# A four-layer graph network: the last LSTMs of two groups of nodes computed together by seven products

## The chip, the cores and the metric

The kernel runs on one core of one Trainium2 chip. The metric is device microseconds from the start to the end of one execution, as the median of several runs.

## The reference

The input x has the shape (128, 64, 256): 128 graphs of 64 nodes with 256 features. All graphs share one adjacency matrix of 64 x 64. Four layers follow each other, each of the form layernorm(x + layer(x)). Layer 0 is a chain of three graph convolutions, layer 1 a convolution in the basis of eigenvectors, layer 3 attention along the edges. Layer 2 holds what is changed:

```python
h = relu(einsum('ts,bsh->bth', adj, x @ Wg0 + bg0))
h = relu(einsum('ts,bsh->bth', adj, h @ Wg1 + bg1))
for p in range(1, 5):
    nw = 64 // p
    wins = h[:, :nw * p, :].reshape(B * nw, p, 256)
    last = lstm_last(Wih[p - 1], Whh[p - 1], bih[p - 1], bhh[p - 1], wins)   # p steps, gates i, f, g, o
    h = h.at[:, arange(nw) * p + (p - 1), :].set(last.reshape(B, nw, 256))
```

So four LSTMs run one after the other on the nodes of a graph. The one with number p takes windows of p neighbouring nodes, runs p steps along each window, and writes its last hidden state over the window's last node. The next one reads what the one before has written. A step multiplies the input, and from the second step on the hidden state too, with a matrix of 256 x 1024, which gives four gates of 256. All of it is done in float32.

## The kernel before

The 8192 rows are cut into 16 groups of 512 rows (8 graphs of 64 nodes). Layer 0 and the eigenvectors come first, for all groups. After them the first stage's memory is given back, the LSTMs' weights are loaded, and layers 1 to 3 run.

For layers 1 to 3, `unit(groups)` writes down the operations of one or two groups: `layer1`, then `to_lstm` with the two convolutions, the four LSTMs, `from_lstm`, and `layer3`. A planner (`Plan.run`) holds up to four units at a time (`UNITS = 4`) and puts their operations into the order of each engine: among the operations that could start earliest by its own table of durations, it takes the one that is due first. The order is fixed when the program is built, and each engine then follows its own list. Work tiles come from pools of fixed size: `WIDE = 7` tiles of 1024 columns (tag `w`), `NARROW = 3` of 512, `GATES = 6` of 1024 for the gates, `CELLS = 3` and `OUTS = 4` of 512 columns for cell state and hidden state (`c`, `hs`), and 8 banks of PSUM. An operation that needs a tile waits in the plan until one is free. When no unit is left to start and `LASTS` groups or fewer are open, TensorE takes the group with the most operations left first.

The units are pairs of groups up to group 12, and then the last four groups one by one (`SINGLE = 4`). The profile counts groups from 1 here: groups 13 to 16 are single units.

In `to_lstm` each group gets its hidden state `hT`, a `w` tile with two halves of 128 features (index k) by 64 nodes by 8 graphs. There are two ways to run an LSTM step.

- `lstm(hT, p, first, nw)` runs one group alone. For each gate and each half of 128 outputs, TensorE sums two products of 128 x 128 by n columns for the input and two for the hidden state in one bank; ScalarE takes the gate's tanh straight from the bank. n is 8 windows' columns: 168 for the third LSTM (21 windows), 128 for the fourth (16 windows).
- `fast(p, n, x, ...)` takes the columns in two halves (index w) and uses seven products in place of eight for each gate, in Winograd's form of Strassen's scheme on 2 x 2 blocks: output halves by feature halves by column halves. VectorE first makes four differences of the inputs (`T1` to `T4`), and the same of the hidden states. The products go to three banks; ScalarE copies three partial sums out of a bank, VectorE adds three more, and then the tanh follow. The weights' sums (`S1` to `S4`) are made once, by `add_weights`.

The first and the second LSTM (`singles`, `pairs`) use `fast` with two halves of one group. The third runs by `lstm(hT, 3, 0, 21)` for each group, the fourth by `four(hTs)` for a pair, which calls `fast` with the two groups as the column halves, and by `lstm(hTs[0], 4, 0, 16)` for a single unit. For the groups in `ENDING`, the last two, `from_lstm` and `layer3` use transposes on TensorE; for the others the data are turned by way of DRAM (`across`).

Of the kernel before, what the change touches and what calls it, by code (L numbers as in the profile page):

```python
# [11 lines left out]
F32 = mybir.dt.float32  # L12
# [740 lines left out]
P = 128  # L753
D = 256
EPS = 1e-5
UNITS = 4
ENDING = (14, 15)
WIDE = 7
NARROW = 3
GATES = 6  # L760
ATT = 2
CELLS = 3
OUTS = 4
LASTS = 3
PERIOD = 17.0
SINGLE = 4
FARS = 8
# [60 lines left out]
def kernel(  # L828
# [346 lines left out]
    for i in range(4):  # L1175
        wih.append(load(wb, f"wih{i}", c_ih[i], "(k p) f -> p k f", [P, 2, 1024], p=P))
        whh.append(load(wb, f"whh{i}", c_hh[i], "(k p) f -> p k f", [P, 2, 1024], p=P) if i else None)
# [31 lines left out]
    def quarters(w):  # L1209
        w = w.rearrange("p k (q h m) -> p k q h m", q=4, h=2)  # L1210
        return [w[:, k, :, h] for h in range(2) for k in range(2)]

    ways = {}
    SPARE21 = {(1, 0), (2, 0), (2, 1)}

    def add_weights(p, ready):
        ways[p] = []
        names = "igo" if p == 1 else "ifgo"
        for k, w in enumerate((wih[p - 1], whh[p - 1])):
            if w is None:  # L1220
                continue
            spare21 = (p, k) in SPARE21
            s = wb.tile([P, 4 - spare21, len(names), P], F32, name=f"sums{p}{k}")
            s, w = plan.tile("sums", [P, 4 - spare21, len(names), P], s), plan.tile("sums", [P, 2, 1024], w)
            whole = quarters(w)
            for at, to in ((slice(0, 1), slice(0, 1)), (slice(2, 4), slice(1, 3))) if p == 1 else ((slice(0, 4),) * 2,):
                a11, a12, a21, a22 = (x[:, at] for x in whole)
                S1, S2, S4, S3 = [s[:, j, to] for j in range(4 - spare21)] + [a21] * spare21
                V.tensor_add(S1, a21, a22, ready=ready)
                V.tensor_sub(S2, S1, a11, ready=ready)  # L1230
                V.tensor_sub(S4, a12, S2, ready=ready)
                V.tensor_sub(S3, a11, a21, ready=ready)
            raw = [{q: x[:, "ifgo".index(q)] for q in names} for x in whole]
            sums = [{q: s[:, j, i] for i, q in enumerate(names)} for j in range(4 - spare21)] + [raw[2]] * spare21
            ways[p].append([raw[0], raw[1], raw[3], sums[0], sums[1], sums[3], sums[2]])

# [14 lines left out]
    def work():  # L1251
        return plan.tile("w", [P, 1024])
# [4 lines left out]
    def ps4(shape=(P, 512)):  # L1257
        return plan.tile("ps", shape)
# [61 lines left out]
    def to_lstm(xs, there):  # L1320
# [19 lines left out]
        pairs(hT)  # L1340
        lstm(hT, 3, 0, 21)
        return hT
# [139 lines left out]

    def lstm(hT, p, first, nw):

        n = 8 * nw
        wi, wh, bias = wih[p - 1], whh[p - 1], cbi[:, p - 1, :]
        hs = None
        for t in range(p):  # L1490
            rows = slice(first + t, first + t + (nw - 1) * p + 1, p)
            xt = [hT[:, k, rows, :] for k in range(2)]
            last = t == p - 1
            names = "figo" if t else "igo"
            gate = []
            for h in range(2):
                G = plan.tile("gates", [P, 1024])[:, :len(names) * n].rearrange("p (q n) -> p q n", n=n)
                gate.append({q: G[:, i] for i, q in enumerate(names)})
            if not t:
                c = plan.tile("c", [P, 512])[:, :2 * n].rearrange("p (h n) -> p h n", h=2)  # L1500
            new = None if last else plan.tile("hs", [P, 512])[:, :2 * n].rearrange("p (h n) -> p h n", h=2)
            for h in range(2):
                for q in names:
                    j = 2 * "ifgo".index(q) + h
                    m = slice(j * P, (j + 1) * P)
                    pp = ps4()[:, :n]
                    ins = [(wi[:, k, m], xt[k]) for k in range(2)]
                    outs = [(wh[:, k, m], hs[:, k, :]) for k in range(2)] if t else []
                    if t and h == 0 and q in names[:2]:

                        run(pp, ins, last=False)
                        run(pp, outs, first=False)
                    else:
                        run(pp, ins + outs)
                    S.activation(gate[h][q], pp, AF.Tanh, bias=bias[:, j:j + 1], scale=0.5 if q == "g" else 0.25)
                    if q == "g":
                        to = gate[h]["g"] if t else c[:, h, :]
                        if t:
                            V.scalar_tensor_tensor(c[:, h, :], gate[h]["f"], 1.0, c[:, h, :], op0=ALU.add,
                                                   op1=ALU.mult)  # L1520
                        V.scalar_tensor_tensor(to, gate[h]["i"], 1.0, gate[h]["g"], op0=ALU.add,
                                               op1=ALU.mult)
                        if t:
                            V.scalar_tensor_tensor(c[:, h, :], c[:, h, :], 0.5, to, op0=ALU.mult, op1=ALU.add)
                        S.activation(gate[h]["i"], c[:, h, :], AF.Tanh, scale=0.5)
                    if q == "o" and not last:
                        V.scalar_tensor_tensor(new[:, h, :], gate[h]["o"], 1.0, gate[h]["i"], op0=ALU.add,
                                               op1=ALU.mult)
            if p == 4 and t == 2:
                plan.late = plan.ops[-1]  # L1530
            if last:

                for h in range(2):
                    V.scalar_tensor_tensor(hT[:, h, slice(first + p - 1, first + nw * p, p), :],
                                           gate[h]["o"].rearrange("p (w b) -> p w b", b=8), 1.0,
                                           gate[h]["i"].rearrange("p (w b) -> p w b", b=8), op0=ALU.add,
                                           op1=ALU.mult)
            hs = new

    def fast(p, n, x, hs=None, c=None, new=None, write=None):  # L1540
# [20 lines left out]
        ins = [x] if first else [x, [[parts(hs[:, k, w]) for w in range(2)] for k in range(2)]]  # L1561
        T = work()[:, :4 * n * len(ins)].rearrange("p (s i n) -> p s i n", s=len(ins), i=4)
        T1, T2, T3, T4 = ([parts(T[:, s, i]) for s in range(len(ins))] for i in range(4))
        for s, b in enumerate(ins):
# [58 lines left out]

    def state(tag):
        return plan.tile(tag, [P, 512]).rearrange("p (h w n) -> p h w n", h=2, w=2)

    def turn_out(dst, o, t):
        V.scalar_tensor_tensor(dst, o.rearrange("p (r b) -> p r b", b=8), 1.0, t.rearrange("p (r b) -> p r b", b=8),
                               op0=ALU.add, op1=ALU.mult)

# [16 lines left out]

    def four(hTs):

        def write(h, o, t):  # L1650
            for w in range(2):
                turn_out(hTs[w][:, h, 3:64:4, :], o[:, w], t[:, w])

        c, hs = state("c"), None
        for t in range(4):
            x = [[hTs[w][:, k, t:t + 61:4, :] for w in range(2)] for k in range(2)]
            new = state("hs") if t < 3 else None
            fast(4, 128, x, hs, c, new, write)
            if t == 2:
                plan.late = plan.ops[-1]  # L1660
            hs = new

    def unit(groups):

        if groups[0] == 0:
            add_weights(1, 10.0)
            add_weights(2, 30.0)
            add_weights(4, 60.0)
        there, hTs = [], []
# [15 lines left out]
        plan.group = groups[0] + 1  # L1685
        if len(groups) == 2:
            four(hTs)
        else:
            lstm(hTs[0], 4, 0, 16)
        late = plan.late  # L1690
# [10 lines left out]

    spare[0] = lambda: tl(few, [P, D], "spare")

    def left_over():
# [54 lines left out]
```

## Time and profile before

| | us |
|---|---|
| median of 3 runs | 2362.1 |
| lowest and highest run | 2360.63, 2365.0 |
| the profiled execution | 2365.63 |
| its span, first to last instruction | 2363.8 |
| TensorE (PE) busy | 2313.2 |
| VectorE (DVE) busy | 1630.6 |
| ScalarE (ACT) busy | 1137.4 |
| mean granted TensorE clock | 0.992 |

In the profile PE is TensorE's matrix product and PEld its weight load. A float32 product of the program shows as two records on PE. Nearly all operations are recorded by helpers, so that most lines read L162 (the planner's `emit`) or L963 (layer 0); groups are told apart by tiles and shapes. "x1408" is the number of records, and the two numbers after a bar are busy microseconds and the mean nanoseconds of one. In the chain and in the timeline the first number of a line is the start in microseconds, the second the duration.

### The profile page before, as it was taken

What the parts mean: (1) busy time and instruction counts of PE and PEld (TensorE: products, weight loads), DVE (VectorE), ACT (ScalarE), POOL (GpSimd) and SP (SyncE); (2) the same over time, 40 slices, a digit from 0 to 9 for tenths busy, and PEclk for the clock granted to TensorE, in tenths of its full rate; (3) what the DMA queues carried; (4) which work ended last, traced back from release to release, by engine and by line L of the source; (5) the groups of instructions that cost most, each with busy time, mean ns of one, the idle gap of its engine ahead of it and who ended that gap; (6) DMA issues with size and microseconds to landing.
All of it is one profiled execution on the core that took longest, in us unless ns stands there. A gap on an engine that the chain in (4) does not pass through costs nothing.

```text
span 2363.8 us, 50357 instructions
## 1 busy us (share of the span) xinstructions
PE 2313.2 (98%) x19872; PEld 2035.5 (86%) x19872; DVE 1630.6 (69%) x5562; ACT 1137.4 (48%) x2838; POOL 142.8 (6%) x315
## 2 busy tenths in 40 slices
PE   8999999999999999999999999999999999999996
PEld 6877888887787778999899899899999998998995
DVE  6888887778898557558567666756755858567535
ACT  2333343333333346555546545545556455545544
POOL 0000000000000010001000100100000101011002
PEclk9999999999999999999999999999999999999998
DMA  7000000000000040002111211220210312222001
GB/s 236 10 1 10 19 10 10 10 10 10 11 10 10 1 161 13 16 11 72 54 42 55 81 51 39 80 65 32 81 43 32 120 48 66 66 92 84 19 1 48
DMA packets 79837, 108.08 MB, mean 46 GB/s; under 512 B 23280, under 2 KB 63984, under 8 KB 79600
## 3 DMA queue, kind: packets, MB, share of 16 engines
q1 hardware_dynamic: 79248, 104.58, 13.3%
q8 instruction: 156, 2.56, 0.4%
q14 instruction: 81, 0.66, 0.1%
q10 hardware_dynamic: 352, 0.28, 0.0%
HBM read 57.90 MB, written 45.09 MB: 44 GB/s over the span
## 4 chain that ended last, share of the span: by engine, by line
PE 92%; DVE 5%; ACT 1%; issue 1%; POOL 0%; DMA 0%; SPq 0%; ACTq 0%; POOLq 0%; DVEq 0%
PE ps L162 60%; PE ps L963 30%; PE ps L1006 2%; DVE D L52 1%; DVE X L162 1%; PE pc L312 1%; DVE w L162 1%; DVE tw L52 0%; DVE st L162 0%; POOL rs L162 0%; DVE gates L162 0%; ACT gates L162 0%; DVE ss L52 0%; DVE v L162 0%; DMA XA<-in_x_dram 0%
## 5 line engine op out<-in xcount | busy, mean ns | idle before, releaser
L162 PE MATMUL ps<-w,wih 128*128 128x128 f32 (+2 forms) x3708 | 649.7, 299 | 3.2 <-DVE gates L162 1.7
L162 PEld LDWEIGHTS ps<-w,wih 128*128 128x128 f32 x3708 | 550.6, 191 | 33.0 <-issue 13.6
L162 ACT ACTIVATE gates<-ps,cbi 128x168 f32<-128x168 f32 (+2 forms) x722 | 261.5, 388 | 207.7 <-PE ps L162 204.1
L162 PE MATMUL ps<-w,sums 128*128 128x128 f32 (+1 forms) x2368 | 353.8, 289 | 3.0 <-ACT gates L162 2.0
L162 PE MATMUL ps<-hs,whh 128*128 128x128 f32 (+1 forms) x1952 | 343.2, 291 | 1.4 <-DVE hs L162 1.4
L162 PEld LDWEIGHTS ps<-w,sums 128*128 128x128 f32 x2368 | 307.6, 192 | 16.6 <-issue 4.3
L162 PEld LDWEIGHTS ps<-hs,whh 128*128 128x128 f32 x1952 | 288.3, 191 | 3.2 <-DVE hs L162 1.8
L162 ACT ACTIVATE gates<-gates,cbi 128x256 f32<-128x256 f32 (+2 forms) x500 | 214.3, 477 | 129.1 <-DVE gates L162 129.0
L162 DVE TENSOR_TENSOR gates<-gates,ps 128x512 f32<-128x512 f32 (+2 forms) x264 | 157.5, 601 | 164.1 <-PE ps L162 157.1
L963 PE MATMUL ps<-aw,h 128*128 128x256 f32 x1024 | 228.2, 380 | 0.0
L963 PEld LDWEIGHTS ps<-aw,h 128*128 128x128 f32 x1024 | 192.6, 190 | 25.9 <-issue 0.4
L162 ACT COPY gates<-ps 128x512 f32<-128x512 f32 (+2 forms) x264 | 136.8, 520 | 160.6 <-PE ps L162 158.8
L972 ACT ACTIVATE h<-h 128x512 f32<-128x512 f32 x128 | 80.6, 630 | 184.4 <-DVE h L52 184.2
L162 DVE SCALAR_TENSOR_TENSOR gates<-gates 128x256 f32<-128x256 f32 (+3 forms) x188 | 78.4, 418 | 69.9 <-ACT gates L162 69.6
L963 PE MATMUL ps<-aw,m 128*128 128x512 f32 x256 | 120.5, 612 | 0.9 <-ACT m L1010 0.9
L963 PE MATMUL ps<-m,aw 128*128 128x256 f32 x512 | 119.7, 387 | 1.0 <-ACT LV L385 0.6
L963 PE MATMUL ps<-ss,tw 128*128 128x256 f32 x512 | 117.8, 379 | 0.1
L963 PE MATMUL ps<-ss,aw 128*128 128x256 f32 x512 | 116.7, 379 | 0.0
L963 PEld LDWEIGHTS ps<-m,aw 128*128 128x128 f32 x512 | 98.1, 194 | 17.3 <-issue 3.0
L162 DVE SCALAR_TENSOR_TENSOR c<-gates,c 128x256 f32<-128x256 f32 (+2 forms) x156 | 56.6, 363 | 76.8 <-ACT gates L162 76.4
L963 PEld LDWEIGHTS ps<-ss,aw 128*128 128x128 f32 x512 | 96.8, 190 | 13.0
L162 POOL TENSOR_SCALAR rs<-mv 128x2 f32<-128x2 f32 x96 | 23.7, 256 | 1390.8 <-DVE mv L162 1372.1
(326 smaller groups left out, 3559.2 us busy)
## 6 DMA issues: line engine op xcount, KB each, us to landing
far<-w SPq DMA_DIRECT2D x42, 512.0 KB, 2.7
w<-far SPq DMA_DIRECT2D x168, 128.0 KB, 3.0
X<-rest SPq DMA_DIRECT2D x24, 512.0 KB, 3.3
out_dram<-X SPq DMA_DIRECT2D x64, 128.0 KB, 1.8
rest<-XA SPq DMA_DIRECT2D x12, 512.0 KB, 2.6
rest<-X SPq DMA_DIRECT2D x12, 512.0 KB, 2.8
XA<-in_x_dram SPq DMA_DIRECT2D x22, 256.0 KB, 6.0
wih<-in_c_ih_dram SPq DMA_DIRECT2D x4, 1024.0 KB, 7.7
```

The costliest lines, as they stand in the source:

```text
L52: return getattr(self.engine, name)(out, *args, **kw)
L162: getattr(e, name)(*[real(x) for x in args], **{k: real(v) for k, v in kw.items()})
L312: PE.matmul(out, lhsT, rhs, start=True, stop=True)
L963: PE.matmul(out, lhsT, rhs, start=start, stop=stop)
L972: S.activation(dst, src, AF.Relu)
L1006: PE.matmul(p[h][m, k, t, :], src[hs, t, f], sqT2[hs, hs], start=True, stop=True)
```

## The change

All 16 groups now form pairs. The third LSTM leaves `to_lstm` and, like the fourth, is run for a pair by `long(hTs, p)`, which calls `fast` with the two groups as the two column halves (n = 168 or 128). `lstm` and `four` are gone. A later step of the third LSTM needs eight differences of 168 columns, more than one `w` tile holds, so `fast` takes two tiles there; with four gates of 168 columns it makes two passes of two gates each. There are nine `w` tiles in place of seven; cell and hidden state tiles are 672 columns wide and there are two of each. `LASTS` is 2 in place of 3. `add_weights` makes sums for all four LSTMs, always three new ones, the fourth in the place of one of the weights' quarters. The unused quarter of the first LSTM's input weights is no longer loaded, which makes two transfers of one. The output that nobody reads of layer 0's normalization (`spare`) goes into the tile of the fourth LSTM's sums.

```diff
-WIDE = 7
+WIDE = 9
-CELLS = 3
-OUTS = 4
-LASTS = 3
+CELLS = 2
+OUTS = 2
+LASTS = 2
-SINGLE = 4
...
+            wih.append(wb.tile([P, 2, 768], F32, name="wih0"))
+            for to, at, n in ((0, 0, 256), (256, 512, 512)):
+                nc.sync.dma_start(wih[0][:, :, to:to + n],
+                                  c_ih[0].rearrange("(k p) f -> p k f", p=P)[:, :, at:at + n])
...
+            s = wb.tile([P, 3, nq, P], F32, name=f"sums{p}{k}")
+            if p == 4:
+                spare[0] = lambda s=s: s[:, 0, 0:2, :].rearrange("p q n -> p (q n)")
...
+            V.tensor_add(S1, a21, a22, ready=ready)
+            V.tensor_sub(S2, S1, a11, ready=ready)
+            V.tensor_sub(S4, a12, S2, ready=ready)
+            V.tensor_sub(a21, a11, a21, ready=ready)
...
         singles(hT)
         pairs(hT)
-        lstm(hT, 3, 0, 21)
         return hT
...
-    def lstm(hT, p, first, nw):
...
-        T = work()[:, :4 * n * len(ins)].rearrange("p (s i n) -> p s i n", s=len(ins), i=4)
-        T1, T2, T3, T4 = ([parts(T[:, s, i]) for s in range(len(ins))] for i in range(4))
+        if 4 * n * len(ins) <= 1024:
+            T = work()[:, :4 * n * len(ins)].rearrange("p (s i n) -> p s i n", s=len(ins), i=4)
+            T = [T[:, s] for s in range(len(ins))]
+        else:
+            T = [work()[:, :4 * n].rearrange("p (i n) -> p i n", i=4) for _ in ins]
+        T1, T2, T3, T4 = ([parts(v[:, i]) for v in T] for i in range(4))
...
-    def state(tag):
-        return plan.tile(tag, [P, 512]).rearrange("p (h w n) -> p h w n", h=2, w=2)
+    def state(tag, n=128):
+        return plan.tile(tag, [P, 672])[:, :4 * n].rearrange("p (h w n) -> p h w n", h=2, w=2)
...
-    def four(hTs):
+    def long(hTs, p):
+
+        nw = 64 // p
+
+        def seen(h, w, t):
+            return hTs[w][:, h, t:t + (nw - 1) * p + 1:p, :]
 
         def write(h, o, t):
             for w in range(2):
-                turn_out(hTs[w][:, h, 3:64:4, :], o[:, w], t[:, w])
-
-        c, hs = state("c"), None
-        for t in range(4):
-            x = [[hTs[w][:, k, t:t + 61:4, :] for w in range(2)] for k in range(2)]
-            new = state("hs") if t < 3 else None
-            fast(4, 128, x, hs, c, new, write)
-            if t == 2:
+                turn_out(seen(h, w, p - 1), o[:, w], t[:, w])
+
+        c, hs = state("c", 8 * nw), None
+        for t in range(p):
+            x = [[seen(k, w, t) for w in range(2)] for k in range(2)]
+            new = state("hs", 8 * nw) if t < p - 1 else None
+            fast(p, 8 * nw, x, hs, c, new, write)
+            if p == 4 and t == 2:
                 plan.late = plan.ops[-1]
             hs = new
...
             add_weights(2, 30.0)
+            add_weights(3, 45.0)
             add_weights(4, 60.0)
...
-        if len(groups) == 2:
-            four(hTs)
-        else:
-            lstm(hTs[0], 4, 0, 16)
+        for p in (3, 4):
+            long(hTs, p)
...
-        units = [(g, g + 1) for g in range(0, NT // 4 - SINGLE, 2)] + [(g,) for g in range(NT // 4 - SINGLE, NT // 4)]
+        units = [(g, g + 1) for g in range(0, NT // 4, 2)]
```

More of the change, by code (lines that the diff above doesn't have):

```diff
@@ L1175 @@
     for i in range(4):
-        wih.append(load(wb, f"wih{i}", c_ih[i], "(k p) f -> p k f", [P, 2, 1024], p=P))
+        if i:
+            wih.append(load(wb, f"wih{i}", c_ih[i], "(k p) f -> p k f", [P, 2, 1024], p=P))
+        else:
[3 more added lines that the diff above has]
+                                  c_ih[0].rearrange("(k p) f -> p k f", p=P)[:, :, at:at + n])
         whh.append(load(wb, f"whh{i}", c_hh[i], "(k p) f -> p k f", [P, 2, 1024], p=P) if i else None)
@@ L1209, in quarters @@
     def quarters(w):
-        w = w.rearrange("p k (q h m) -> p k q h m", q=4, h=2)
+        w = w.rearrange("p k (q h m) -> p k q h m", h=2, m=P)
         return [w[:, k, :, h] for h in range(2) for k in range(2)]
     ways = {}
-    SPARE21 = {(1, 0), (2, 0), (2, 1)}
     def add_weights(p, ready):
@@ L1221, in add_weights @@
                 continue
[L1222 to L1235, printed above, removed]
+            nq = len(names)
+            s = wb.tile([P, 3, nq, P], F32, name=f"sums{p}{k}")
+            if p == 4:
+                spare[0] = lambda s=s: s[:, 0, 0:2, :].rearrange("p q n -> p (q n)")
+            s, w = plan.tile("sums", [P, 3, nq, P], s), plan.tile("sums", [P, 2, nq * 2 * P], w)
+            a11, a12, a21, a22 = whole = quarters(w)
+            S1, S2, S4 = (s[:, j] for j in range(3))
+            V.tensor_add(S1, a21, a22, ready=ready)
+            V.tensor_sub(S2, S1, a11, ready=ready)
+            V.tensor_sub(S4, a12, S2, ready=ready)
+            V.tensor_sub(a21, a11, a21, ready=ready)
+            raw = [{q: x[:, i] for i, q in enumerate(names)} for x in whole]
+            sums = [{q: s[:, j, i] for i, q in enumerate(names)} for j in range(3)]
+            ways[p].append([raw[0], raw[1], raw[3], *sums[:2], raw[2], sums[2]])
     def products(calls, also=(), **kw):
@@ L1481, in layer3 @@
                 Q.dma_start(out_t[:, at + j, :], x2[:, j, :])
-    def lstm(hT, p, first, nw):
[L1487 to L1512, printed above, removed]
-                    else:
[L1514 to L1538, printed above, removed]
@@ L1561, in fast @@
         ins = [x] if first else [x, [[parts(hs[:, k, w]) for w in range(2)] for k in range(2)]]
-        T = work()[:, :4 * n * len(ins)].rearrange("p (s i n) -> p s i n", s=len(ins), i=4)
-        T1, T2, T3, T4 = ([parts(T[:, s, i]) for s in range(len(ins))] for i in range(4))
+        if 4 * n * len(ins) <= 1024:
+            T = work()[:, :4 * n * len(ins)].rearrange("p (s i n) -> p s i n", s=len(ins), i=4)
+            T = [T[:, s] for s in range(len(ins))]
+        else:
+            T = [work()[:, :4 * n].rearrange("p (i n) -> p i n", i=4) for _ in ins]
+        T1, T2, T3, T4 = ([parts(v[:, i]) for v in T] for i in range(4))
         for s, b in enumerate(ins):
@@ L1622, in fast @@
                             write(h, g, gate[h]["i"])
-    def state(tag):
-        return plan.tile(tag, [P, 512]).rearrange("p (h w n) -> p h w n", h=2, w=2)
+    def state(tag, n=128):
+        return plan.tile(tag, [P, 672])[:, :4 * n].rearrange("p (h w n) -> p h w n", h=2, w=2)
     def turn_out(dst, o, t):
-        V.scalar_tensor_tensor(dst, o.rearrange("p (r b) -> p r b", b=8), 1.0, t.rearrange("p (r b) -> p r b", b=8),
-                               op0=ALU.add, op1=ALU.mult)
+        o, t = (v.rearrange("p (r b) -> p r b", b=8) for v in (o, t))
+        V.scalar_tensor_tensor(dst, o, 1.0, t, op0=ALU.add, op1=ALU.mult)
     def singles(hT):
@@ L1685, in unit @@
         plan.group = groups[0] + 1
-        if len(groups) == 2:
-            four(hTs)
-        else:
-            lstm(hTs[0], 4, 0, 16)
+        for p in (3, 4):
+            long(hTs, p)
         late = plan.late
@@ L1700, in unit @@
                 layer3(x, g, 0, 4)
-    spare[0] = lambda: tl(few, [P, D], "spare")
     def left_over():
```

## The prediction

> **What bounds the kernel now.** I read the page first (busy shares, slices, chain), then the groups by form, the chain in order of time, the timeline of TensorE, and busy time by stretch.
>
> ```profile
> PE 2313.2 (98%) x19872; PEld 2035.5 (86%) x19872; DVE 1630.6 (69%) x5562; ACT 1137.4 (48%) x2838; POOL 142.8 (6%) x315
> ...
> PE   8999999999999999999999999999999999999996
> ...
> PE 92%; DVE 5%; ACT 1%; issue 1%; POOL 0%; DMA 0%; SPq 0%; ACTq 0%; POOLq 0%; DVEq 0%
> ```
>
> TensorE is busy in nearly every slice but the last and makes 92% of the chain that ended last. So a product taken out of the order counts in full, as long as something is ready to take its place. The groups by form show what is taken out of the third LSTM: 1408 + 1024 = 2432 records of 168 columns, two for each product of the program.
>
> ```profile
> L162 PE MATMUL ps<-w,wih 128*128 128x168 f32 x1408 | 238.8, 306 | 0.0
> ...
> L162 PE MATMUL ps<-hs,whh 128*128 128x168 f32 x1024 | 181.4, 306 | 0.0
> ```
>
> Their mean of 306 ns is no price, because records overlap; the price is the distance from start to start in dense stretches of the timeline:
>
> ```profile
> 1001.24 1.87 PE L162 MATMUL ps<-hs,whh 128*128 128x168 f32 x12
> 1002.95 1.17 PE L162 MATMUL ps<-w,wih 128*128 128x256 f32 x6
> ...
> 2267.51 6.41 PE L162 MATMUL ps<-w,wih 128*128 128x128 f32 x56
> 2273.76 1.06 PE L162 MATMUL ps<-hs,whh 128*128 128x128 f32 x8
> ```
>
> (1002.95 - 1001.24)/12 = 0.1425 us for a record of 168 columns, (2273.76 - 2267.51)/56 = 0.1116 us for one of 128: a product costs 0.285 or 0.223 us.
>
> Busy time by stretch shows the side engines, the chain shows the end:
>
> ```profile
> core 0: us, PE busy (x) PEld busy (x) DVE busy (x) ACT busy (x) POOL busy (x), PEclk, DMA share, GB/s
> ...
> 600.00:700.00 100.00, 99.19 (x774) 79.45 (x773) 89.87 (x301) 35.70 (x80) 4.17 (x10) 1.00 0.03 12
> ...
> 2200.00:2300.00 100.00, 100.00 (x777) 98.06 (x776) 40.98 (x119) 54.23 (x156) 0.00 (x0) 1.00 0.02 6
> 2300.00:2363.80 63.80, 45.02 (x355) 38.32 (x353) 34.97 (x125) 29.74 (x76) 12.15 (x36) 0.86 0.14 44
> ```
>
> ```profile
> 2176.40 141.68 PE ps L162 x1140
> ```
>
> From 2176 to 2318 us TensorE never waits: there the LSTMs of groups 15 and 16, two separate units, fill each other's waits. Then comes a tail of 46 us in which TensorE is half idle.
>
> **The change part by part.**
>
> (1) Third LSTM. Before, a group has 12 + 32 + 32 = 76 products, a pair 152. By seven products a pair has 21 + 56 + 56 = 133. Eight pairs: 8 x 19 = 152 products less, x 0.285 = 43.3 us.
>
> (2) Fourth LSTM of the last four groups. Two groups alone have 2 x (12 + 3 x 32) = 216, a pair 21 + 3 x 56 = 189. Two pairs: 54 x 0.223 = 12.0 us. Together 55.3 us; no other product changes in number.
>
> [...] if weight loads set the pace, every product, wide or narrow, is worth one narrow product: (152 + 54) x 0.223 = 46 us in place of 55.3. But with the same weight load a record of 168 columns takes 0.031 us longer than one of 128, so the columns set the pace, and I keep 55.3.
>
> (3) Work moved to VectorE and ScalarE, from rows of before (sizes without a row between their neighbours: 0.50 us for a VectorE operation on 336, 0.57 for a tanh of 336, 0.44 for a copy of 336). VectorE, third LSTM: 320 x 0.33 = 105 us becomes 176 state operations, 120 adds of banks and 160 differences = 199 us; fourth: +23; sums of the third's weights 8 x 0.68 = 5. In all +122 us, so VectorE goes from some 66% of the stretch after 900 us to 76%. ScalarE: third 173 to 202, fourth +5, so from 55% to about 60%. Both stay under TensorE, and at 90% VectorE (600 to 700 us above) it still ran at 99%. On the path: nothing by itself; through later releases, see (4).
>
> (4) New waits between steps. Two chains of a pair become one: the third LSTM waits for both groups, and each of its steps, and of the fourth's, waits for the state of the one before. From the last but one product of a step to the first of the next: the add from the bank (0.68), three tanh at their spacing of 0.43 (1.30 for three in the timeline), two state operations (0.42 each, one hidden), tanh of the cell (0.42), the output (0.42): about 3.3 us, and 4.6 where ScalarE first takes three tanh from the bank. Cover is what TensorE is given in between. In the built program's order pairs 1 to 7 have 3.3 to 27 us of other products at each of the six places. Two places matter: first to second step of the fourth LSTM, 3.3 to 3.9 us for a need of 2.9 (three gates), and of the third, 4.3 to 7.4 for 3.3. So they are hidden, if barely. State tiles fall from three and four to two and two, which holds back the second LSTM of the next pair; that is in the order already. I put 3 us on the middle; ends 0 and 15 (8 pairs x 6 x 0.3).
>
> (5) The last pair has no pair behind it. Its covers are 2.3, 4.6, 4.6, 3.1, 3.6 and 1.8 us. Against the needs of (4): 1.0 + 0 + 0 + 0 + 1.1 + 2.8 = 5 us idle, where before the 141.68 us had none. Ends: 0, and 20 (six bare places at 3.3).
>
> (6) The clock. The trace shows what such waits can cost more:
>
> ```profile
> 1969.04 0.70 PE L162 MATMUL ps<-w,wih 128*128 128x256 f32 x2 [1.72 <-DVE gates L162]
> ...
> 1970.34 1.52 PE L162 MATMUL ps<-w,wih 128*128 128x128 f32 x6 [0.60 <-DVE w L162]
> ```
>
> ```profile
> 1968.00:1972.00 4.00, 2.36 (x16) 0.80 0.32 131
> 1972.00:1976.00 4.00, 4.00 (x84) 0.77 0.67 205
> ```
>
> Two waits of 1.72 and 0.60 us within 3 us brought some 3.4 us at half clock (PEclk is the column after the instruction counts: shares of 0.20 and 0.23 missing from 4 us each, over 0.5). [...] by the row the one of 2.8 us does, 1.7 us, and perhaps another. I follow the row: +2, ends 0 and 12 [...].
>
> (7) Gone with the single units: the waits around 1967 to 1982 us, where the first single unit starts alone (1.72 + 0.60 + 0.89 in the timeline, and the 1.7 of clock): -4; ends -5 and 0.
>
> (8) The tail. Both groups now leave the fourth LSTM together, and nothing stands between its last product and the transposes: eight tanh, two cells, output and copies, some 4.4 us bare (before, the last group's gate of 128 columns and a product of group 14 covered this). On the other side the 25 VectorE operations of group 14's attention that stood in the tail (some 10 us at 0.42) are done before it; in a tail where VectorE has 35 of 64 us about half of them lay on the chain. 0; ends -6 and +6.
>
> (9) Start. The first layer's weights come in two transfers without a quarter that nobody reads; eight sums more on VectorE, hidden by the first groups' products. The activation's throw-away output now lies in the tile of the fourth's sums, which are made after it. 0; ends 0 and +5. Loads of rows and results of all groups keep their number on SP's queue, and POOL's operations theirs; for the last pair the two reloads of rows follow each other after the fourth LSTM's third step, 12.5 us of products ahead of their use, against 3.3 us to land.
>
> Sum: -55.3 + 3 + 5 + 2 - 4 + 0 + 0 = -49.3 us. On the profiled execution, 2365.6 us (its span 2363.8 and 1.8 around it), that gives 2316.3. That execution is 3.5 us above the median of the runs, 2362.1; on the median: 2312.8, so 2313 us.
>
> **The rivals.** *The joint chain sets the pace* (slower than before). Place: the steps of third and fourth LSTM in every pair. Price: six places at 2.8 us bare, 8 x 6 x 2.8 = 134 us, so 2362 - 55 + 134 = 2441 us. It decides from 55.3/8 = 6.9 us of waiting a pair, three bare places of six. For it: two state tiles each, six gate tiles of which one step of the third LSTM takes four, and covers within 1 us of the need. Against it: before's pairs had covers down to 4.1 us in the same order and TensorE waited there for less than 1 us a time. 4%.
>
> *The last pair and its clock cost more*: every place of the last pair is bare [...]: 20 + 12 in place of 7, and 10 more in the middle, so 2313 + 35 = 2348 at the end; its middle 2332 us. For it: the rows of (6). Against it: needs that were summed from durations include most of the hand-over. 21%.
>
> *More than the sum*: the waits of (4) and (5) are hidden and the tail shortens by 6 us: 2362 - 55 - 4 - 6 = 2297 to 2304. 10%.
>
> *The change doesn't take the products out*: the built order has 1064 products of 168 columns (1216 before) and 1512 of 128 in the fourth LSTM (1566 before), as counted in (1) and (2). 0%.
>
> **How the numbers follow.** My forecast, 2304 to 2324 us, has 65%; the costly last pair 21%, more than itself 10%, slower 4%. The range 2302 to 2336 leaves out the far ends of the two side cases and the slow one, 2 in 10. Runs of this kernel lie within 0.2% (2360.6 to 2365.0), about what can be told from no change; faster by more than that 0.95, within it 0.01, slower 0.04.
>
> **What would show it.** Right: records of 168 columns 2128 and not 2432; TensorE's busy time down by about 55 us; no long wait of TensorE between 950 and 2150 us; three to five waits of 1 to 3 us on hs in the last 120 us before the tail. Wrong: waits on hs, c or gates of over 1 us that come back every 175 us (the joint chain); a granted clock under 1 in the last LSTM for over 5 us (the costly last pair); VectorE over 90% where TensorE waits.

## Result: 2320.9 us, 1.75% faster, 8 us above the forecast

| | before | after |
|---|---|---|
| median of four runs each, us | 2361.63 | 2320.89 |
| lowest and highest | 2360.63, 2365.0 | 2320.49, 2321.7 |
| profiled execution | 2365.63 | 2321.25 |
| its span | 2363.8 | 2319.4 |

The ratio is 0.9825, with a 95% interval of 0.9808 to 0.9842. The forecast was 2313, its range 2302 to 2336. From the page of the kernel after, the engines' busy time, TensorE's slices and the chain's shares:

```profile
PE 2264.2 (98%) x19460; PEld 1979.4 (85%) x19460; DVE 1725.3 (74%) x5730; ACT 1156.6 (50%) x2800; POOL 142.0 (6%) x315
...
PE   8999999999999999999999999999999999999996
...
PE 89%; DVE 7%; issue 1%; ACT 1%; POOL 1%; DMA 1%; SPq 0%; ACTq 0%; DVEq 0%; POOLq 0%
```

TensorE is still the engine that sets the time; 412 records are gone, and VectorE's part of the chain that ended last grew from 5 to 7%. The groups by form, records of 168 columns, after:

```profile
L162 PE MATMUL ps<-w,wih 128*128 128x168 f32 x704 | 148.9, 308 | 2.2 <-DVE gates L162 1.6 <-ACT gates L162 0.4
L162 PE MATMUL ps<-w,sums 128*128 128x168 f32 x784 | 129.8, 308 | 5.3 <-DVE w L162 5.3
L162 PE MATMUL ps<-hs,whh 128*128 128x168 f32 x256 | 57.4, 306 | 0.0
L162 PE MATMUL ps<-w,whh 128*128 128x168 f32 x256 | 57.4, 306 | 0.0
L162 PE MATMUL ps<-hs,sums 128*128 128x168 f32 x128 | 28.7, 306 | 0.0
```

They sum to 2128, as counted. Before, no group of 168 columns had a wait ahead of it; now the products with `sums` wait 5.3 us for VectorE. That is the first sign of what the forecast missed. The waits of TensorE between 900 and 2140 us (what was waited for: us in total, times, longest), before:

```profile
PE ps L162 <- ACT gates L162: 2.0, 3, 0.7
PE ps L162 <- DVE gates L162: 1.7, 1, 1.7
PE ps L162 <- ACT w L162: 1.6, 3, 0.5
PE ps L162 <- DVE hs L162: 0.9, 1, 0.9
PE ps L162 <- ACT v L162: 0.7, 1, 0.7
PE ps L162 <- DVE w L162: 0.6, 1, 0.6
```

And after:

```profile
PE ps L162 <- DVE w L162: 5.9, 4, 2.4
PE ps L162 <- DVE gates L162: 0.8, 3, 0.3
PE ps L162 <- ACT gates L162: 0.4, 1, 0.4
```

The view lists waits from 0.15 us on. None for `hs` or `c` is among those after: the steps of pairs 1 to 7 are covered. The wait for `w` is another matter. The timeline of VectorE and TensorE after, at its longest place, and the same place on SP's queue (SPq; `far<-w` is the write of a round trip through DRAM, `w<-far` one of its four reads):

```profile
1461.56 5.53 SPq L162 DMA_DIRECT2D far<-w  x3
1467.20 8.06 SPq L162 DMA_DIRECT2D w<-far  x12
...
1476.29 0.69 DVE L162 TENSOR_TENSOR X<-w,X 128x512 f32<-128x512 f32 x1 [2.75 <-DMA w<-far]
...
1477.77 0.32 DVE L162 TENSOR_TENSOR w<-w,w 128x168 f32<-128x168 f32 x1
...
1478.15 1.67 PE L162 MATMUL ps<-w,sums 128*128 128x168 f32 x6 [2.38 <-DVE w L162]
```

Three round trips through DRAM (`across`) meet on one queue. VectorE stands in its fixed order for 2.75 us ahead of an addition whose rows are not back; behind it in the order is a difference of the third LSTM (1477.77), and TensorE waits 2.38 us for that. A VectorE at 74% delays TensorE here not because it is busy but because it is in order. The same wait comes back near 1659 and 1838 us, with 1.74 and 1.22 us. Behind the first one clock is missing too, in busy time by stretch (PEclk is the 0.57, so 1.7 of the 4 us are missing):

```profile
1478.00:1482.00 4.00, 3.85 (x18) 3.85 (x19) 3.02 (x9) 1.62 (x4) 0.00 (x0) 0.57 0.02 5
```

In the last pair, the timeline of TensorE after has four waits before the hand-over, then three in the tail:

```profile
2156.11 1.60 PE L162 MATMUL ps<-w,wih 128*128 128x256 f32 x8 [0.51 <-DVE gates L162]
...
2190.40 1.41 PE L162 MATMUL ps<-w,wih 128*128 128x168 f32 x8 [0.87 <-DVE gates L162]
...
2244.45 0.49 PE L162 MATMUL ps<-w,wih 128*128 128x128 f32 x2 [1.80 <-DVE gates L162]
...
2261.77 0.49 PE L162 MATMUL ps<-hs,whh 128*128 128x128 f32 x2 [2.27 <-DVE hs L162]
...
2277.49 0.44 PE L162 MATMUL ps<-ident,w 128*128 128x128 f32 x1 [3.18 <-DVE w L162]
2278.29 3.46 PE L162 MATMUL ps<-ident,w 128*128 128x128 f32 x15 [0.35 <-ACT w L162]
2285.36 2.16 PE L162 MATMUL ps<-ident,X 128*128 128x128 f32 x8 [3.61 <-ACT X L162]
```

The first four are 5.45 us in sum, where the forecast had 5; the one of 0.51 us, ahead of 256 columns, is of neither the third nor the fourth LSTM. The 3.18 us are the hand-over of both groups to the transposes with nothing under it. Before, the same stretch was filled with a product of group 14:

```profile
2315.75 1.88 PE L162 MATMUL ps<-w,dw 128*128 128x512 f32 x4
2317.47 1.47 PE L162 MATMUL ps<-ident,w 128*128 128x128 f32 x12
...
2326.11 2.16 PE L162 MATMUL ps<-ident,X 128*128 128x128 f32 x8 [5.45 <-ACT X L162]
```

### The profile page after: what moved, and what is told of

Its sections match the earlier page's. It is cut to its first block, busy times and chain, and to the rows that moved or that the text cites. A ratio compares the mean times of both kernels' runs of the same rounds, so it can differ in the third digit from the quotient of the medians.

```text
span 2319.4 us, 49711 instructions
## 1 busy us (share of the span) xinstructions
PE 2264.2 (98%) x19460; PEld 1979.4 (85%) x19460; DVE 1725.3 (74%) x5730; ACT 1156.6 (50%) x2800; POOL 142.0 (6%) x315
## 4 chain that ended last, share of the span: by engine, by line
PE 89%; DVE 7%; issue 1%; ACT 1%; POOL 1%; DMA 1%; SPq 0%; ACTq 0%; DVEq 0%; POOLq 0%
PE ps L162 55%; PE ps L962 31%; PE ps L1005 2%; DVE w L162 1%; POOL rs L162 1%; DVE X L162 1%; DVE D L52 1%; DMA w<-far 1%; DVE st L162 1%; DVE gates L162 1%; PE pc L312 1%; ACT gates L162 0%; DVE tw L52 0%; SPq L162 0%; DMA aw<-in_a_w_dram 0%
## 5 line engine op out<-in xcount | busy, mean ns | idle before, releaser
L162 PE MATMUL ps<-w,sums 128*128 128x128 f32 (+2 forms) x3104 | 477.0, 294 | 6.4 <-DVE w L162 6.4
L162 PEld LDWEIGHTS ps<-w,sums 128*128 128x128 f32 x3104 | 420.3, 191 | 23.8 <-DVE w L162 7.7
L162 ACT ACTIVATE gates<-gates,cbi 128x256 f32<-128x256 f32 (+4 forms) x736 | 314.7, 480 | 195.9 <-DVE gates L162 193.2
L162 DVE TENSOR_TENSOR gates<-gates,ps 128x512 f32<-128x512 f32 (+4 forms) x408 | 235.7, 583 | 191.9 <-PE ps L162 182.6
L162 ACT COPY gates<-ps 128x512 f32<-128x512 f32 (+4 forms) x408 | 205.0, 508 | 240.4 <-PE ps L162 236.7
L162 PE MATMUL ps<-hs,whh 128*128 128x128 f32 (+1 forms) x896 | 181.2, 284 | 2.3 <-DVE hs L162 2.3
L162 PE MATMUL ps<-w,whh 128*128 128x128 f32 (+1 forms) x896 | 181.1, 284 | 0.0
L162 PEld LDWEIGHTS ps<-hs,whh 128*128 128x128 f32 x896 | 139.7, 191 | 2.5 <-DVE hs L162 2.5
L162 ACT ACTIVATE gates<-ps,cbi 128x128 f32<-128x128 f32 (+2 forms) x368 | 119.8, 386 | 42.1 <-PE ps L162 41.0
L162 PEld LDWEIGHTS ps<-w,whh 128*128 128x128 f32 x896 | 139.7, 191 | 0.0
```

The source lines that it names most:

```text
L162: getattr(e, name)(*[real(x) for x in args], **{k: real(v) for k, v in kw.items()})
```

## Experiments

All are read with one measure. Each TensorE record from the first one of layers 1 to 3 on (column *start*) is priced at its distance from start to start in dense stretches: 0.1425 us for 168 columns, 0.1116 for 128, 0.2155 for 256, 0.4293 for 512, 0.0362 and 0.0178 for the two small shapes. The sum is the *work*; time minus work is the *lag*, which holds every wait, every stretch of low clock and every record that starts a little late. The span is cut where 154 us of work are left, roughly where the last pair is alone: ahead of it is the *middle*, behind it the *end*.

| kernel | time, us | span | start | middle: work | middle: lag | end: lag |
|---|---|---|---|---|---|---|
| before | 2361.63 | 2363.8 | 847.0 | 1304.5 | 33.5 | 24.9 |
| before, nine tiles | 2356.37 | 2354.7 | 847.1 | 1304.5 | 24.9 | 24.2 |
| fourth in pairs, seven tiles | 2365.59 | 2365.9 | 849.1 | 1292.4 | 34.5 | 35.9 |
| fourth in pairs, nine tiles | 2352.86 | 2350.8 | 847.4 | 1292.4 | 22.0 | 35.0 |
| **after** (third too, nine tiles) | 2320.89 | 2319.4 | 846.6 | 1249.1 | 34.9 | 34.9 |
| after, eight tiles | 2340.85 | 2337.6 | 846.1 | 1249.1 | 51.1 | 37.2 |
| after, seven tiles | 2444.43 | 2442.4 | 849.2 | 1249.1 | 152.7 | 37.3 |
| after, seven tiles, single units | 2432.77 | 2431.7 | 848.6 | 1272.0 | 134.6 | 22.5 |

Time is the median of several runs; the other columns are one execution of each kernel, and the middle's lag of one and the same order differed by some 3 us between executions (shown below). The runs beside them of the kernel before had medians of 2361.6 to 2364.7, so ratios are given where a few microseconds matter.

**How many work tiles.** The change with seven tiles, as many as before:

```diff
-WIDE = 9
+WIDE = 7
```

> The changed kernel with seven large work tiles instead of nine. Theory (the products are what is gained, tiles only keep the next pair's products at hand): up to 8 us slower than the changed kernel, 2321 to 2329 us. Rival (the nine tiles carry the change: with seven a pair that holds four tiles in the third LSTM starves the next pair): the six places between steps become bare, 8 pairs x 6 x 2.8 us, and most of the gain is gone, 2360 us or more.

Measured 2444.43 us, ratio 1.0343 [1.0326, 1.0359]: slower than before, and my theory fell. The rival's range holds the time, but its reason, bare steps, is the smaller part: TensorE waits 7.2 us in sum for `hs` and 7.0 for `gates`. Its largest wait in sum with seven tiles, and the longest single one with SP's queue:

```profile
PE ps L162 <- DMA w<-far: 48.1, 8, 15.9
...
1376.73 0.38 SPq L162 DMA_DIRECT2D far<-w  x1
1381.68 0.79 SPq L162 DMA_DIRECT2D w<-far  x2
1382.53 5.10 SPq L162 DMA_DIRECT2D att<-v  x8
1387.67 1.06 SPq L162 DMA_DIRECT2D w<-far  x2
...
1391.44 2.04 PE L162 MATMUL ps<-w,att 128*128 128x256 f32 x4 [15.90 <-DMA w<-far]
```

TensorE stands 15.9 us, in order, ahead of a product of layer 3 whose rows take a round trip through DRAM; the trip's last two reads even stand behind eight other transfers. The order built with seven tiles has nothing else ahead of that product. The waits for `w<-far` are some 48 of the 118 us of added lag in the middle. The mean granted clock is lower too, 0.975 for 0.991 with nine tiles, so 61 us of full clock are missing from the span for 21 (how much of that falls into waits is not shown).

With eight:

```diff
-WIDE = 9
+WIDE = 8
```

> The changed kernel with eight work tiles; nine gave 2321, seven 2444. Theory (each tile less makes products of layer 3 stand before rows that come back from DRAM, in fewer places than with seven): 2335 to 2380, with waits of TensorE for w<-far of 10 to 40 us in sum. Rival (a threshold: eight are enough, only seven are too few): under 2330, no wait for w<-far over 1 us.

Measured 2340.85 us, ratio 0.9902 [0.9889, 0.9916]. TensorE waits 10.7 us in two places for `w<-far` and once 6.1 for `att<-v`. The theory holds: the loss fades with each tile, 124, 20, and it lies in the middle (lag 152.7, 51.1, 34.9).

**Nine tiles in the kernel before.**

```diff
-WIDE = 7
+WIDE = 9
```

> The kernel before with nine work tiles in place of seven and nothing else. Theory (before's TensorE waits for no tile, so tiles alone give nothing): 2360 to 2366. Rival (tiles alone are worth part of the gain): under 2352.

Measured 2356.37 us, ratio 0.9969 [0.9959, 0.9979]. It fits neither the theory nor the rival: tiles alone give 0.3%, some 7 us. In the table it is nearly all middle, 33.5 to 24.9. The waits of TensorE between 900 and 2140 us are now

```profile
PE ps L162 <- DVE hs L162: 1.8, 1, 1.8
PE ps L162 <- DVE w L162: 0.3, 1, 0.3
```

The six short waits for `gates` and `w` that before had (2.0 + 1.6 us, one of each some 183 us apart) are gone, and so is the one of 1.7 us near 1969, behind which 1.7 us of clock were missing. Why two more tiles build an order without them was not taken apart. I had taken before's own waits as given.

**The fourth LSTM in pairs alone**, third as before, with seven tiles:

```diff
-SINGLE = 4
+SINGLE = 0
```

> The kernel before with its last four groups in pairs and nothing else: third LSTM by group with eight products, fourth of all pairs by seven. Theory (54 products less are 12.0 us; the last pair's fourth LSTM runs bare, some 5 us between its steps and 2 of clock): 2361.6 - 12 + 7 = 2357 us, with waits on hs and gates near the end that the kernel before does not have. Rival (the last pair's waits cost as much as its products save): 2361 us or more. Second rival (nothing is lost at the end): 2350 us.

Measured 2365.59 us, ratio 1.0004 [0.9995, 1.0013]: the rival. The work fell by the 12 us reckoned, the end took 11.0 more and the middle 1.0. In this execution layers 1 to 3 also began 2.1 us later, which is all that the spans differ by.

The same with nine tiles, made from the kernel after:

```diff
         pairs(hT)
+        lstm(hT, 3, 0, 21)
...
-            add_weights(3, 45.0)
...
-        for p in (3, 4):
-            long(hTs, p)
+        long(hTs, 4)
```

> The changed kernel with nine work tiles, fourth LSTM of all groups in pairs by seven, but the third LSTM of each group by itself and by eight products, as before the change: 152 products of 168 columns more. Theory (with nine tiles each product counts in full): 152 x 0.285 = 43.3 us more than 2321, less at most 5 for the two separate chains that cover each other at the end: 2359 to 2365, TensorE waiting nowhere for w<-far. Rival (the nine tiles by themselves are worth part of the gain, the products only the rest): under 2350.

Measured 2352.86 us, ratio 0.9953 [0.9939, 0.9966]: below the theory's lower end and above the rival's, as seven of the microseconds come from the tiles. Between 900 and 2140 us TensorE has no wait that the view lists. The step from here to the kernel after is the third LSTM's: spans 2350.8 to 2319.4, 31.4 us, for 1292.4 - 1249.1 = 43.3 us of work. Of its products, 12 us came back as lag, and all of that in the middle (22.0 to 34.9).

**The third LSTM in pairs with single units at the end**, with seven tiles: eight products need the weights' quarter that the sums overwrite, and a fourth sum for it takes room:

```diff
-WIDE = 9
+WIDE = 7
...
+SINGLE = 4
...
-        units = [(g, g + 1) for g in range(0, NT // 4, 2)]
+        units = [(g, g + 1) for g in range(0, NT // 4 - SINGLE, 2)] + [(g,) for g in range(NT // 4 - SINGLE, NT // 4)]
```

> The third LSTM in pairs for groups 1 to 12 only; groups 13 to 16 are single units with third and fourth LSTM by eight products, as before (seven large work tiles, since the weights' quarters must be kept beside their sums). Theory (every product taken out of the order counts in full; a few microseconds come back as waits in the middle): 6 pairs x 19 products x 0.285 = 32.5 us less than before, and some 5 us of waits: 2334 us. Rival (the joint chain of a pair costs waiting in every pair): under half of the 32.5 us arrives, 2346 us or more.

Measured 2432.77 us, ratio 1.0289 [1.0272, 1.0306]. The time lies in the rival's range, but not for its reason: seven tiles cost over 100 us by themselves, so as a test of what a pair costs the run failed. Against the run with seven tiles and all pairs it still says one thing: with 22.9 us more work (1272.0 against 1249.1 in the middle) it is 11.7 faster: its end lags by 14.8 us less (22.5 for 37.3) and its middle by 18.1 less.

**Planning landings later.** The planner adds 3.0 us to each transfer on SP's queue until its data may be used:

```diff
-    LAG = {"PE": 0.205, "DVE": 0.13, "ACT": 0.14, "POOL": 0.0, "SP": 3.0}
+    LAG = {"PE": 0.205, "DVE": 0.13, "ACT": 0.14, "POOL": 0.0, "SP": 4.5}
```

> The changed kernel with one number of the planner changed: it counts on 4.5 us instead of 3.0 from the issue of a transfer to the use of what it brings, so operations that wait for a transfer stand later in VectorE's order. Theory (three waits of TensorE of 1.4 to 2.4 us near 1478, 1659 and 1838 us come from VectorE standing before an addition whose rows have not landed, with the LSTM's differences queued behind it): those 5.7 us and the 1.7 us of clock near 1480 go, 2314 us. Rival (VectorE is late with the differences anyway, being at 74%): the waits stay or move, 2319 to 2325 us.

Measured 2322.48 us, ratio 0.9823 [0.9809, 0.9838]: the rival. In place of the three waits stand three of 0.56 us ahead of other products, and waits for `gates` (2.0 us in two places), `hs` (0.7) and `mv` (0.4) came. The lag of the middle stayed at 34.7.

A narrower form changes only the planned cost of a round trip's read:

```diff
-                        seen(far[:, 256 * j:256 * j + 256], "(i r) f -> r i f", i=4), cost=0.45)
+                        seen(far[:, 256 * j:256 * j + 256], "(i r) f -> r i f", i=4), cost=0.7)
```

> The changed kernel with 0.7 us in place of 0.45 as the planner's cost of one of the four reads of a round trip through DRAM (w<-far), which is what such a read took on SP's queue where three round trips met (8.06 us for twelve); only the order changes: two writes (far<-w) with no read between them are left in four places, not eight. Theory (the three waits near 1478, 1659 and 1838 us and the half clock after the first come from reads that share SP's queue, ahead of which VectorE stands in order): they go, 5 to 8 us less, 2313 to 2317. Rival (as with the later landings planned for all of SP, the waits only move): 2319 to 2324.

Measured 2317.32 us (2316.53 to 2319.27), ratio 0.9802 [0.9787, 0.9817]. The waits of TensorE between 900 and 2140 us:

```profile
PE ps L162 <- DVE gates L162: 1.2, 1, 1.2
PE ps L162 <- DVE w L162: 0.6, 1, 0.6
```

The three waits are gone, and the half clock after the first (PEclk is 1.00 from 1476 to 1482 us, where the kernel after has 0.50 from 1479 to 1482); the middle's lag fell from 34.9 to 26.5, by 8.4. The theory names 7.0 of it (2.38 + 1.74 + 1.22 us of waits and 1.7 of clock). The end gave 2.6 back (37.5), so the time lies just above the theory's upper end.

How much of the 8.4 us belongs to the order, the traces of three other runs tell. The runs of the last pair below have the order of the kernel after on every engine up to 1994 us. There their three waits sum to 3.8, 4.5 and 4.1 us, for 5.3 in the kernel after, and up to that place they lag by 30.1 to 31.0 us, where the kernel after lags by 33.4 and this run by 25.1. So the order is worth 5 to 8 us, and up to 3 us are a matter of the one execution.

And with 0.9:

> The changed kernel with 0.9 us as the planner's cost of a read (0.45 in it, 0.7 in the run before). The middle of the order is nearly that of 0.7; the last pair's covers become 5.2, 4.6, 4.6, 1.9, 3.6 and 5.3 us (0.7: 4.0, 4.6, 4.6, 3.1, 3.6, 1.8). Theory (reads that share SP's queue made the middle's waits; cover against need makes the last pair's): no wait of over 1 us between 1200 and 2100 us; the wait of 2.4 us for hs ahead of the last step is gone, and a wait of about 1 us more for gates comes ahead of the second step of the fourth LSTM: 2314 to 2318. Rival (0.7 was a lucky order, the waits of the middle come back): 2319 to 2325.

Measured 2316.07 us (2314.25 to 2316.29), ratio 0.9799 [0.9786, 0.9813]. The middle lags by 26.2, and between 1200 and 2100 us no wait is over 1 us; its order there is close to that of 0.7, so this is a weak second draw of an order. The wait for `hs` ahead of the last step is gone; for gates TensorE waits 3.8 us in four places (3.6 in three with 0.7), none over 1.2, and the wait expected ahead of the second step came, with 0.93, while the one a step later shrank from 1.81 to 1.06. The end lags by 35.0. No run lies as high as the lowest of the change (2320.49), though the two ratios' intervals touch at their ends: this is the best version found, by some 0.2%.

**The last pair.** An order in which the last step of its fourth LSTM has more under it:

```diff
-LASTS = 2
+LASTS = 1
```

> The changed kernel with LASTS 1 in place of 2: the rule that lets the group with most work left go first, whatever its due time, begins only when one group is left and not two. In the built order that alters the last pair: before the last step of its fourth LSTM TensorE now has 3.6 us of other products in place of 1.8, all other places being the same. Theory (cover against need sets these waits): the wait of 2.3 us for hs ahead of that step is gone or under 0.7, and the time is 1 to 4 us less, 2317 to 2320. Rival (what is gained there comes back in the tail, whose order alters too): 2321 to 2326 with the wait gone just the same.

Measured 2321.76 us, ratio 0.9822 [0.9808, 0.9835]. The wait for `hs` is gone, so cover against need does set it; the time is unchanged, the rival. The end's lag is 37.3, with waits for `att` in the tail of 3.6 us in place of 0.3.

The last pair's two groups apart in the fourth LSTM:

```diff
-        for p in (3, 4):
-            long(hTs, p)
+        long(hTs, 3)
+        lates = []
+        if groups[-1] < NT // 4 - 1:
+            long(hTs, 4)
+        else:
+            for w in raws:
+                a11, _, a21, _ = quarters(w)
+                V.tensor_sub(a21, a11, a21)
+            for g, hT in zip(groups, hTs):
+                plan.group = g + 1
+                lstm(hT, 4, 0, 16)
+                lates.append(plan.late)
...
```

> The changed kernel, but the two groups of the last pair go through the fourth LSTM apart, each by eight products, as the single units did before; two subtractions put back the quarter that the sums had overwritten. 27 products of 128 columns more, 6.0 us. Their last steps end some 4 us apart, so one group's products lie under the other's hand-over to the transposes. Theory (what the end lost by the change is the common last step and its hand-over): the wait before the transposes falls from 3.3 to under 1.5 us, the tail after the last LSTM product and the waits of the last pair give back 4 to 8: 2318 to 2323. Rival (the loss lies in the tail's own chain, not in the hand-over): 2325 to 2329.

Measured 2332.1 us, ratio 0.9864 [0.9849, 0.9879]: slower than theory and rival had it. The hand-over is as the theory had it, from the timeline of TensorE:

```profile
2286.75 0.61 PE L162 MATMUL ps<-hs,whh 128*128 128x128 f32 x4
2287.40 0.30 PE L162 MATMUL ps<-ident,w 128*128 128x128 f32 x1
2288.36 2.27 PE L162 MATMUL ps<-ident,w 128*128 128x128 f32 x15 [0.65 <-ACT w L162]
2294.81 2.17 PE L162 MATMUL ps<-ident,X 128*128 128x128 f32 x8 [4.19 <-ACT X L162]
```

No wait of 3.18 us stands ahead of the transposes any more, and the end's lag falls from 34.9 to 29.9. But these 5.0 us are less than the 6.0 of products that they cost, and the middle took 7.3 more (lag 42.2): from 1994 us on the order differs from that of the kernel after, so the planner arranges the pair before the last otherwise too, and behind that place the middle lags by 11.2 us for 1.5. I had reckoned with neither.

With group 15 first, on top of the run before:

```diff
-LASTS = 2
+LASTS = 1
```

> As the run with the last pair apart, and LASTS 1 in place of 2, so that group 15 goes through its fourth LSTM first and group 16 fills in: 15's layer 3 then lies beside 16's steps. Same products. Theory (the tail is long because both groups reach it together): 2315 to 2320, TensorE idle less after the last LSTM product. Rival (16's steps alone are bare, and each bare step costs what the tail gains): 2322 to 2330, with waits for gates and hs in the last 50 us of the LSTM.

Measured 2332.99 us, ratio 0.9867 [0.9851, 0.9884]: above theory and rival too. The end lags by 31.1, no better. The middle's loss (lag 41.8) is the same, so these two runs tell what the hand-over is worth and not what the best end would be.

## Why the forecast was nearly right, step by step

The product counts were exact, and the two large errors behind them, the tiles and the middle's waits, almost cancelled. That part of the hit is luck.

- *(1) and (2), products.* Right: the work fell by 55.4 us (1304.5 to 1249.1), for the 55.3 forecast. Records of 168 columns still start 0.1425 us apart where they run dense (two pairs at 1309.40 and 1309.69 us), and those of 128 with the same weight load of 128 x 128 0.1116, so the columns set the pace, as said. The 46 us of a pace set by weight loads are near the 44.4 that the spans differ by, but not for that reason: the difference is lag, most of whose places the traces show. Busy time fell by 49.0, not 55: of the 11.4 us of added lag only 4.6 are idle time (span less busy time is 50.6, then 55.2), the rest lies within busy time.
- *Not in the sum: the two more work tiles.* The prediction named the covers that the built order has, and never asked what the tiles do to before's own waits. Nine tiles alone took 9.1 us of span, 7 on the ratio, nearly all from the middle. Without them the change would have been slower than before by 3.4%.
- *(3), VectorE and ScalarE.* Right: summed record by record, VectorE's durations rose by 119.5 us for +122 and ScalarE's by 33.6 for +34. Busy time rose less, by 94.7 and 19, because it counts records that overlap once. Off the path in sum, as said; not in order, see (4).
- *(4), waits in the middle: the step that failed.* Forecast 3 us, ends 0 and 15. Against the kernel that differs only in the third LSTM the middle lags by 12.9 us more (22.0 to 34.9). None of it is a wait between steps for `hs` or `c`, which is what (4) priced. Some 8.4 us of it went with the planned cost of a read: round trips that share SP's queue, with VectorE in order behind them (up to 3 of these are the one execution). Of the 4.5 us that remain (22.0 to 26.5), 0.9 are waits of 0.15 us and more; the rest are records that start late by less, 2.3 us of it between two records of 168 columns, where some 25 starts come 0.1 us late. What holds those was not looked into.
- *(5), the last pair's covers.* Right in the waits: 0.87, 1.80 and 2.27 us, 4.94 in sum, for 1.0, 1.1 and 2.8. Two are over 1 us, one on `hs` and one on `gates`, where the text expected three to five on `hs`. Too small as a price: from the line between middle and end to the last LSTM product the lag grew by 8.2 us (0.4 to 8.5), and 2.6 of it lie in no wait that the view lists.
- *(6), clock.* The 2 us stood for the last pair, where the granted clock stayed at 1.00 through the waits of 1.80 and 2.27 us; it was behind the middle's wait of 2.38 us that 1.7 were missing, in this execution. That the sum came out is luck: the section at the end has one wait with and without that loss.
- *(7), the single units' waits.* Right in direction: with all groups in pairs and nine tiles the middle lost 2.9 us of lag (24.9 to 22.0), forecast 4. But of the waits named, the 1.72 and 0.60 us were already gone with nine tiles and single units; what pairing took were a wait of 1.8 us for `hs` and one of 0.3.
- *(8), the tail.* Nearly right: 0, and 1.8 us came. The bare hand-over cost 3.3 us more than before. From there to TensorE's last record the lag fell by 5.5 (17.4 to 11.8): TensorE's waits for `X` and `att`, 5.45 and 5.41 us before, are 3.61 and 0.29. So the balance of hand-over and tail came out, but not surely for the reason given: single units with seven tiles have 4.20 and 0.29 as well. And from TensorE's last record to the end it now takes 11.2 us, not 7.2, which the sum had not looked at. With the 8.2 of (5) this makes the 10.0 by which the end's lag grew (24.9 to 34.9). In the table, every kernel whose last two groups are a pair has an end of 34.9 us or more, every one with single units 22.5 to 24.9, whatever its tiles.
- *(9), the start.* Right: layers 1 to 3 begin within 0.4 us of before. (Over the kernels of the table this start moves by 3 us.)

The sum on the profiled execution: work -55.4, middle +1.4, end +10.0, start -0.4 (846.6 for 847.0 us) make the -44.4 us measured, against -49.3. That is 4.9 of the miss. The rest, 3.1 us, is that the forecast took before's profiled execution, 3.5 above its median, as the measure for after's, which lay 0.4 above.

Of the rivals, *the joint chain sets the pace* did not happen: between 900 and 2140 us TensorE never waits for `hs` or `c`; the waits that come back every 180 us are for `w`. A time like its 2441 us did arise with seven tiles, but by transfers, not by bare steps. *The last pair and its clock cost more* was right on the end's direction (10 us for the forecast's 7) and wrong on size and clock. *More than the sum* did not happen.

## What to carry over

When a change takes work off the engine that sets the time, ask of everything that comes with it (here two tiles) what it does to the old kernel and what the change is without it; two runs answered that, one with 7 us, as much as the forecast's error, the other with 124. A side engine at 74% can still hold up the first one if it stands in a fixed order ahead of a transfer (2.75 us ahead of one, and TensorE waited 2.38): read what is queued behind each of its waits, and check the planner's cost of a transfer against the queue in the trace where several meet. The last unit has nothing behind it, so joining its two groups saves products and pays at the end: the fourth LSTM's 12 us of products came with some 11 us of lag there.

## What the runs showed of the hardware

The length of a wait did not tell in these runs what the granted clock was behind it. The same wait in the same place, 2.27 us for `hs` ahead of the last step, ends at 2261.77 us in the kernel after and at 2256.54 us in the run with the read cost 0.7. Busy time by stretch from about there on (PEclk is the column after the counts), in the kernel after

```profile
2261.00:2266.00 5.00, 4.23 (x37) 4.23 (x38) 2.88 (x10) 1.41 (x4) 0.00 (x0) 1.00 0.00 0
```

and in the run with 0.7

```profile
2257.00:2262.00 5.00, 5.00 (x33) 5.00 (x32) 1.25 (x6) 0.92 (x2) 0.00 (x0) 0.66 0.00 0
```

So no clock is missing in the first, and 1.7 of the 5 us in the second. What decides between the two is not shown. In the kernel after, the clock was 1.00 too in the 5 us behind the waits of 1.74, 1.22 and 1.80 us, and 0.57 in the 4 us behind the one of 2.38 us. Before, around the waits of 1.72 and 0.60 us near 1969, it was 0.80 and then 0.77 in 4 us each. So in this case a wait of some 2 us could only be given a range as its price in clock, from 0 to 1.7 us.

A read of a round trip takes SP's queue 0.43 us (the median of 168, before and after). Where three trips meet, twelve take 8.06 us; ten of them take 0.30 to 0.46 each, two take 0.78 and 1.46, and 1.8 us lie between them. So 0.67, the mean, is no duration of a read, and a planned cost of 0.7 works as room for such places.
